# Context keys and values of a decoder layer: seven-product projections on two positions side by side, 512 columns each, and values turned by VectorE when they are loaded

## The chip, the cores and the metric

The kernel runs on one core of one Trainium2 chip. The metric is device time in microseconds (us) for one execution. The engines are named as in the profile: PE (TensorE, matrix products; PEld is its loading of the stationary operand), DVE (VectorE), ACT (ScalarE), POOL (GpSimd), SP (SyncE, which here issues most transfers). SBUF is the memory on the core, PSUM the memory that PE writes its sums to.

## What is computed

One decoder layer over 8 positions t of 512 rows each: self-attention across the positions, cross-attention to a context, and a small network, each followed by an addition and a layer norm. The change concerns the context's keys and values:

```python
x = layernorm(x + self_attention(x, ...))                    # 8 positions x 512 rows x 512
# cross-attention: ctx is 8 x 512 rows x 1024 features
src_trans = einsum('bsf,of->bso', ctx, W_src) + b_src        # W_src: 1024 x 1024
src_trans = src_trans * mask[:, :, None]
k, v = split(src_trans, 2, axis=2)                           # 8 heads of 64
q = (einsum('btf,of->bto', x, W_tgt) + b_tgt) * mask[:, :, None]
scores = where(mask == 0, -inf, einsum('bthd,bshd->bhts', q, k) / 8)
update = einsum('bhts,bshd->bthd', softmax(scores), v)
x = layernorm(x + einsum('btf,of->bto', concat(x, update), W_out) + b_out)
x = layernorm(x + network(x))                                # rounded to a small float format
```

All data that concern the change are 32-bit floats.

## The kernel before

**Two halves.** The first half (to line 617) does self-attention and the context's keys and values; the second half does cross-attention and the network. They meet in DRAM: normalized rows in `x1d`, keys in `kd`, values in `vd`, one tensor for each position.

**First half, main work.** A loop over j, four blocks of 128 rows; in each block all 8 positions t. PE projects keys, queries and values (`ps_k`, `ps_q`, `ps_v`, line 338) from `xt`, and a bias term `bd` (line 369). DVE forms the scores (lines 379 and 388, `pq` and `sc`) and the weighted values (lines 428 to 444, `pv` and `ao`). PE turns the result (`aot`, line 449) and applies the output projection (`po`, line 454). The input rows are loaded again into `r` (line 463, pool `rp`, 5 buffers), POOL adds a bias, DVE adds `po`, takes statistics and normalizes four positions at a time, and ACT's queue stores the rows to `x1d`.

**First half, context products.** For positions 0 to 6 the projection is done with seven block products in place of eight (lines 482 to 617). W_src's half for keys (part 0) or for values (part 1) is cut in 2 x 2 blocks, 256 outputs by 512 features. The context of one position, transposed (features on partitions), is cut in 2 x 2 blocks as well: `cl` and `ch`, the lower and the upper 512 features, by two halves of 256 rows. `halves` loads four blocks of W_src into one tile `w` and DVE forms three sums in it (`sums_of_a`, lines 136 to 139). `context_of` loads `cl` and `ch`, DVE forms the sums `tx` (`sums_of_b`, lines 142 to 145), and in part 0 the sums are stored to DRAM (`td`), so that part 1 loads them and doesn't form them again. In part 0 the stationary operand is a block of `w` and 256 columns of context move, giving keys transposed. In part 1 the stationary operand is a block of context and 256 columns of `w` move, giving values with rows on partitions. `product` (line 535) makes four matmuls over the four feature chunks. Three banks `py`, `pz`, `px` take the sums; ACT (`put`) writes a bank to the staging tile `st`, adding the bias or multiplying by the mask, and DVE (`add`) adds another bank to it (lines 587 and 589). The order of the seven products is A12, S1, A11, S2, S4, S3, A22. The staging tiles go to `kd` and `vd` from ACT's queue.

The scheduler mixes these products with the main work by its own estimates; on each engine the resulting order is fixed. Position 7 is projected plainly (`project_context`, eight groups of eight matmuls, lines 151 to 187), by a matrix `w_src` that is loaded at the start of the second half.

**Buffers that matter.** `big` holds one tile: `w` of part 0, then `w` of part 1, then `w_src`, then the network's `w1`. A tile can be loaded when the last reader of the one before it is done. `cxp` has 10 buffers of 2 KB a partition for `cl` and `ch`, 8 for each position; `tcp` has 5 of 3 KB for `tx`, 4 for each position. `kst` has 4 staging buffers, `ps_kv` three PSUM banks.

**Second half.** Here the order on PE, DVE, ACT and SP is written out by hand: `weave` sets steps of attention between dense products, and smaller works of DVE wait in the lists `urgent` and `side`, which `run` empties by a credit as PE's steps go by. A list `later` holds loads that go out a number of steps later. For each position t and each of four column chunks c (two heads), `scores` makes the scores (line 782), DVE and ACT form the softmax (lines 797 to 822), DVE turns 32x32 blocks into `pb` (line 834), sixteen transfers on SP's queue put these in place as `pT` (line 847), and `attend` multiplies by the values `v` (line 881). `load_v` fetches the values of one chunk with one transfer, two chunks ahead (`kvd` has 2 buffers). `queries`, `project_x1`, `project_u`, `hidden` and `finish` are the dense products.

Of the kernel before, what the change touches and what calls it, by code (L numbers as in the profile page):

```python
# [42 lines left out]
def decoder_layer(  # L43
# [145 lines left out]
    with ExitStack() as ph:  # L189
# [136 lines left out]
        rp = ph.enter_context(tc.tile_pool(name="rp", bufs=5))  # L326
        sm = ph.enter_context(tc.tile_pool(name="sma", bufs=2))
        cxp = ph.enter_context(tc.tile_pool(name="cxp", bufs=10))
        tcp = ph.enter_context(tc.tile_pool(name="tcp", bufs=5))
# [17 lines left out]
        for j in range(NJ):  # L347
# [134 lines left out]
        HF, W2 = FC // 2, S // 2  # L482
        td = [
            [dram.tile([P, 5, W2], F32, name=f"td{t}_{f}") for f in range(HF)]
            for t in range(T - 1)
# [13 lines left out]
        def context_of(t, part):  # L499
            lo, hi, tx = [], [], []  # L500
            for f in range(HF):
                a = cxp.tile([P, S], F32, tag="ct", name=f"cl{part}{t}_{f}")
                b = cxp.tile([P, S], F32, tag="ct", name=f"ch{part}{t}_{f}")
                x = tcp.tile([P, 3, W2], F32, tag="tx", name=f"tx{part}{t}_{f}")
                nc.sync.dma_start(b, ctxT[t, (HF + f) * P : (HF + f + 1) * P, :])
                if part == 0:
                    nc.sync.dma_start(a, ctxT[t, f * P : (f + 1) * P, :])
                    with tc.high_priority():
                        sums_of_b(
                            nc.vector,  # L510
                            *(u[:, h * W2 : (h + 1) * W2] for u in (a, b) for h in (0, 1)),
                            *(x[:, i] for i in range(3)),
                        )
                    nc.sync.dma_start(td[t][f][:, 0:2], a)
                    nc.sync.dma_start(td[t][f][:, 2:5], x)
                else:
                    nc.sync.dma_start(a, td[t][f][:, 0:2])
                    nc.sync.dma_start(x, td[t][f][:, 2:5])
                lo.append(a)
                hi.append(b)  # L520
                tx.append(x)
            return lo, hi, tx

        for part in range(2):
            w7 = halves(part)
            for t in range(T - 1):
                lo, hi, tx = context_of(t, part)
                first, second = slice(0, W2), slice(W2, S)
                b11, t3 = [u[:, first] for u in lo], [u[:, second] for u in lo]
                b21, b22 = [u[:, first] for u in hi], [u[:, second] for u in hi]  # L530
                t1, t2, t4 = ([u[:, i] for u in tx] for i in range(3))
                for i in range(2):
                    ps = slice(i * P, (i + 1) * P)

                    def product(bank, a, b, start):


                        for f in range(HF):
                            nc.tensor.matmul(  # L539
                                bank[:, first],  # L540
                                lhsT=w7[:, a, f, ps] if part == 0 else b[f][:, ps],
                                rhs=b[f] if part == 0 else w7[:, a, f, :],
# [5 lines left out]
                    def bank(name):  # L548
                        return ps_kv.tile(
                            [P, S], F32, tag="kv", name=f"{name}{part}{t}_{i}"  # L550
# [3 lines left out]
                    st = [  # L554
                        kst.tile([P, S], F32, tag="st", name=f"st{part}{t}_{i}_{k}")
                        for k in range(2)
                    ]
                    at = {}
                    for r in range(2):
                        for c in range(2):  # L560
                            k, q = (r, c) if part == 0 else (c, r)
                            at[r, c] = k, st[k][:, (first, second)[q]]

                    def put(r, c, src):


                        k, dst = at[r, c]
                        n = i + 2 * k
                        with tc.high_priority():
                            if part == 0:  # L570
                                nc.scalar.activation(
                                    dst, src[:, first], AF.Identity, bias=col(C_BK + n)
                                )
                            else:
                                nc.scalar.activation(
                                    dst,
                                    src[:, first],
                                    AF.Copy,
                                    scale=maskcol[:, t, n : n + 1],
                                )  # L580

                    def add(r, c, src):
                        k, dst = at[r, c]
                        n = i + 2 * k
                        with tc.high_priority():
                            if part == 0:
                                nc.vector.tensor_tensor(dst, src[:, first], dst, ALU.add)
                            else:
                                nc.vector.scalar_tensor_tensor(
                                    dst,  # L590
                                    src[:, first],
                                    maskcol[:, t, n : n + 1],
                                    dst,
                                    ALU.mult,
                                    ALU.add,
                                )
# [9 lines left out]
                    add(0, 0, x)  # L606
                    product(x, S2, t2, False)
                    put(0, 1, x)
                    product(z, S4, b22, False)
                    add(0, 1, z)  # L610
                    product(x, S3, t3, False)
                    add(1, 1, x)
                    product(x, A22, t4, False)
                    put(1, 0, x)
                    for k in range(2):
                        d = (kd, vd)[part][t]
# [683 lines left out]
```

## Time and profile before

| | |
|---|---|
| three runs, median (lowest to highest) | 2162.68 us (2159.54 to 2164.2) |
| the profiled execution, its own time | 2161.87 us |
| its span, first to last instruction | 2160.1 us |
| L539, context products | 1568 records, 366.6 us busy |
| L338, `ps_k`, `ps_q`, `ps_v` | 768 records, 342.3 us busy |
| L428, DVE, weighted values | x64, mean 2320 ns |
| L834, DVE, 32x32 turns | x256, mean 678 ns |
| L143, DVE, a sum of context, 256 columns | x28, mean 607 ns |
| mean granted PE clock | 0.989 |

The profile is of one execution. A stage is a stretch of the span in microseconds from its start. For each engine the busy time in a stage is given; PEclk is the clock granted to PE as a share of full speed; the DMA share is that of the core's 16 DMA engines. An f32 product stands as two records. The last `po` of the first half ends at 873.6 us, the last context product at 922.9, and the first query product of the second half starts at 922.7.

### The profile page before, as it was taken

What the parts mean: (1) busy time and instruction counts of PE and PEld (TensorE: products, weight loads), DVE (VectorE), ACT (ScalarE), POOL (GpSimd) and SP (SyncE); (2) the same over time, 40 slices, a digit from 0 to 9 for tenths busy, and PEclk for the clock granted to TensorE, in tenths of its full rate; (3) what the DMA queues carried; (4) which work ended last, traced back from release to release, by engine and by line L of the source; (5) the groups of instructions that cost most, each with busy time, mean ns of one, the idle gap of its engine ahead of it and who ended that gap; (6) DMA issues with size and microseconds to landing.
All of it is one profiled execution on the core that took longest, in us unless ns stands there. A gap on an engine that the chain in (4) does not pass through costs nothing.

```text
span 2160.1 us, 19078 instructions
## 1 busy us (share of the span) xinstructions
PE 2080.1 (96%) x6544; PEld 1040.1 (48%) x6544; DVE 1453.5 (67%) x2378; ACT 479.8 (22%) x1011; POOL 143.7 (7%) x124
## 2 busy tenths in 40 slices
PE   7999999999999999997899999999999999999998
PEld 5564665466446666742343444444443434343443
DVE  3799998999999989255663574754735638456232
ACT  2012111110211121122223233232232322323211
POOL 1000110011001101000000001000010000000000
PEclk9999999999999999998999999999999999999999
DMA  8130343044324224984495572744744628336200
GB/s 287 67 127 15 134 172 132 6 141 151 93 67 158 88 98 146 283 232 130 105 211 123 107 143 72 131 113 98 132 117 99 145 67 147 103 83 141 64 20 20
DMA packets 253297, 257.48 MB, mean 119 GB/s; under 512 B 141456, under 2 KB 161936, under 8 KB 253200
## 3 DMA queue, kind: packets, MB, share of 16 engines
q1 hardware_dynamic: 236976, 227.65, 41.7%
q10 hardware_dynamic: 16224, 28.61, 3.6%
q8 instruction: 52, 0.85, 0.2%
q14 instruction: 45, 0.37, 0.1%
HBM read 129.84 MB, written 59.24 MB: 88 GB/s over the span
## 4 chain that ended last, share of the span: by engine, by line
PE 75%; DVE 16%; DMA 5%; issue 1%; SPq 1%; ACT 1%; POOL 0%; ACTq 0%; DVEq 0%
PE h L970 21%; PE px L539 7%; PE pox L915 5%; PE av L881 5%; PE s L782 5%; PE pox L903 5%; PE psq L762 4%; PE o L987 4%; DVE pv L428 4%; PE pz L539 4%; PE ps_q L338 3%; PE po L454 2%; DVE pv L438 2%; DVE sc L388 2%; DVE pq L379 2%; PE py L539 2%
## 5 line engine op out<-in xcount | busy, mean ns | idle before, releaser
L970 PE MATMUL h<-x2T,w 128*128 128x512 f32 x1024 | 454.7, 599 | 4.5 <-DVE x2T L726 4.5
L970 PEld LDWEIGHTS h<-x2T,w 128*128 128x128 f32 x1024 | 192.2, 191 | 263.4 <-issue 253.9
L797 DVE CUSTOM_DVE_ANT_0 pe<-s,mb 128x512 f32<-128x512 f32 x256 | 162.0, 682 | 218.2 <-PE s L782 218.2
L807 ACT ACTIVATE pe<-pe,nmax 128x512 f32<-128x512 f32 x256 | 182.2, 712 | 217.6 <-DVE nmax L797 215.7
L834 DVE STREAM_TRANSPOSE pb<-pe 128x512 f32<-128x512 f32 x256 | 159.6, 678 | 0.0
L977 ACT ACTIVATE hq<-h,colv 128x512 fp8e4<-128x512 f32 x128 | 88.0, 687 | 302.4 <-PE h L970 302.4
L428 DVE TENSOR_TENSOR pv<-v,sc 128x2048 f32<-128x2048 f32 x64 | 148.5, 2320 | 2.0
L379 DVE TENSOR_TENSOR pq<-qw,k 128x2048 f32<-128x2048 f32 x64 | 146.6, 2291 | 1.1
L388 DVE TENSOR_REDUCE sc<-pq 128x64 f32<-128x2048 f32 x64 | 146.0, 2281 | 1.4
L782 PE MATMUL s<-kT,qTx 64*128 64x512 f32 x512 | 128.9, 620 | 4.3 <-DVE nmax L797 4.1
L881 PE MATMUL av<-pT,vx 128*64 128x512 f32 x512 | 119.2, 608 | 8.9 <-DMA pT<-pb 8.9
L762 PE MATMUL psq<-x1Ts,w_tgt 128*128 128x512 f32 x256 | 117.0, 610 | 5.8 <-DVE x1Ts L726 5.8
L822 DVE TENSOR_SCALAR pe<-pe,rden 128x512 f32<-128x512 f32 x256 | 116.9, 499 | 4.5
L454 PE MATMUL po<-w_o,aoT 128*128 128x512 f32 x256 | 117.4, 601 | 0.8 <-ACT aoT L451 0.8
L338 PE MATMUL ps_q<-w_in,xt 128*128 128x512 f32 x256 | 116.8, 594 | 0.0
L915 PE MATMUL pox<-w_xo,uT 128*128 128x512 f32 x256 | 115.2, 598 | 0.0
L903 PE MATMUL pox<-w_xo,x1Ts 128*128 128x512 f32 x256 | 114.4, 595 | 0.0
L987 PE MATMUL o<-w2q,hq 128*128 128x512 fp8e4 x512 | 114.1, 379 | 0.0
L338 PE MATMUL ps_k<-w_in,xt 128*128 128x512 f32 x256 | 113.9, 593 | 0.1
L338 PE MATMUL ps_v<-w_in,xt 128*128 128x512 f32 x256 | 111.6, 594 | 0.0
L922 DVE TENSOR_TENSOR x<-pox,x 128x512 f32<-128x512 f32 x32 | 22.1, 692 | 107.9 <-PE pox L915 60.2
L900 POOL TENSOR_TENSOR x<-x,bxo 128x512 f32<-128x512 f32 x32 | 39.9, 1279 | 817.7 <-DMA x<-x1d 318.6
(153 smaller groups left out, 2397.3 us busy)
## 6 DMA issues: line engine op xcount, KB each, us to landing
pT<-pb SPq DMA_DIRECT2D x512, 128.0 KB, 2.3
ch<-in_ctxT_dram SPq DMA_DIRECT2D x56, 256.0 KB, 3.4
td<-tx SPq DMA_DIRECT2D x28, 384.0 KB, 3.2
tx<-td SPq DMA_DIRECT2D x28, 384.0 KB, 5.0
r<-in_x_dram SPq DMA_DIRECT2D x32, 256.0 KB, 3.6
xt<-in_xT_dram SPq DMA_DIRECT2D x32, 256.0 KB, 2.7
x1d<-r ACTq DMA_DIRECT2D x32, 256.0 KB, 3.5
x1Ts<-x1d SPq DMA_DIRECT2D x32, 256.0 KB, 5.9
```

What stands on the lines that cost most here:

```text
L338: nc.tensor.matmul(ps, lhsT=xt[:, e, :], rhs=w_in[:, e, part * E : (part + 1) * E], start=(e == 0), stop=(e == EC - 1),)
L379: nc.vector.tensor_tensor(pr, qw[:, fs] .rearrange("p (h d) -> p h d", d=D1) .unsqueeze(2) .to_broadcast([P, HH, T, D1]), k_all[:, :, fs]. ...
L388: nc.vector.tensor_reduce(sc[:, t, g * HH * T : (g + 1) * HH * T], pr.rearrange("p h s d -> p (h s) d"), AX.X, ALU.add,)
L428: nc.vector.tensor_tensor(pr, v_all[:, :, fs].rearrange("p s (h d) -> p s h d", d=D1), sc[:, t, g * HH * T : (g + 1) * HH * T] .rearrange( ...
L539: nc.tensor.matmul(bank[:, first], lhsT=w7[:, a, f, ps] if part == 0 else b[f][:, ps], rhs=b[f] if part == 0 else w7[:, a, f, :], start=st ...
L762: nc.tensor.matmul(ps, lhsT=w_tgt[:, e, o * P : (o + 1) * P], rhs=x1T[t][:, e, :], start=(e == 0), stop=(e == EC - 1),)
L782: nc.tensor.matmul(ps[:, h, :], lhsT=qT[t][half[h], c, j * P : (j + 1) * P], rhs=kT[t, c][half[h], :], start=True, stop=True,)
L881: nc.tensor.matmul(av[half[h], :], lhsT=v[t, c][:, s, half[h]], rhs=pT[t, c][:, :, :, s, h].rearrange("p g i q -> p (g i) q"), start=(s == 0),
L903: nc.tensor.matmul(po, lhsT=x1T[t][:, e, j * P : (j + 1) * P], rhs=w_xo[:, e, :], start=(e == 0), stop=False,)
L915: nc.tensor.matmul(po, lhsT=uT[t][:, e, j * P : (j + 1) * P], rhs=w_xo[:, EC + e, :], start=False, stop=(e == EC - 1),)
L970: nc.tensor.matmul(ps, lhsT=w1[0][:, e, n * P : (n + 1) * P], rhs=x2T[t][:, e, :], start=(e == 0), stop=(e == EC - 1),)
L987: nc.tensor.matmul(po, lhsT=hq[t][:, c, j * P : (j + 1) * P], rhs=w2q[:, c, :], start=(c == 0), stop=(c == HC - 1),)
```

## The change

- Positions 0 to 5 are taken in three pairs. The 2 x 2 blocks of context are now the lower and upper features by the two positions of a pair, so every product moves 512 columns. There are 336 of them, where there were 784 with 256 columns.
- In part 1, too, the stationary operand is a block of `w`. Values therefore come out transposed, like the keys, with features on partitions and rows as columns, and are stored so. When a bank is written to `st`, its 32-column blocks are reordered.
- Every result block has a staging tile of its own (four for each step, from the same four buffers) and is stored when it is complete.
- The mask and the turning of the values move to the second half: `load_v` fetches a raw chunk in four transfers, `turn_v` has DVE turn 32x32 blocks and POOL multiply by the mask. The work is put in the list `side`, one chunk ahead.
- Position 6 is projected plainly like position 7, at the end of the first half, by `w_src`, whose load moves there from the second half.
- `cxp` has 8 buffers of twice the size and `tcp` 4 of twice the size, one pair's worth each; `rp` has 4.

```diff
-        rp = ph.enter_context(tc.tile_pool(name="rp", bufs=5))
+        rp = ph.enter_context(tc.tile_pool(name="rp", bufs=4))
...
-        cxp = ph.enter_context(tc.tile_pool(name="cxp", bufs=10))
-        tcp = ph.enter_context(tc.tile_pool(name="tcp", bufs=5))
+        cxp = ph.enter_context(tc.tile_pool(name="cxp", bufs=8))
+        tcp = ph.enter_context(tc.tile_pool(name="tcp", bufs=4))
...
-        def context_of(t, part):
+        def context_of(m, part):
...
-                a = cxp.tile([P, S], F32, tag="ct", name=f"cl{part}{t}_{f}")
-                b = cxp.tile([P, S], F32, tag="ct", name=f"ch{part}{t}_{f}")
-                x = tcp.tile([P, 3, W2], F32, tag="tx", name=f"tx{part}{t}_{f}")
-                nc.sync.dma_start(b, ctxT[t, (HF + f) * P : (HF + f + 1) * P, :])
+                a = cxp.tile([P, 2, S], F32, tag="ct", name=f"cl{part}{m}_{f}")
+                b = cxp.tile([P, 2, S], F32, tag="ct", name=f"ch{part}{m}_{f}")
+                x = tcp.tile([P, 3, S], F32, tag="tx", name=f"tx{part}{m}_{f}")
...
+                nc.sync.dma_start(b, two(HF + f))
...
-            for t in range(T - 1):
-                lo, hi, tx = context_of(t, part)
-                first, second = slice(0, W2), slice(W2, S)
-                b11, t3 = [u[:, first] for u in lo], [u[:, second] for u in lo]
-                b21, b22 = [u[:, first] for u in hi], [u[:, second] for u in hi]
+            for m in range(PAIRS):
+                lo, hi, tx = context_of(m, part)
+                b11, t3 = [u[:, 0] for u in lo], [u[:, 1] for u in lo]
+                b21, b22 = [u[:, 0] for u in hi], [u[:, 1] for u in hi]
...
-                                bank[:, first],
-                                lhsT=w7[:, a, f, ps] if part == 0 else b[f][:, ps],
-                                rhs=b[f] if part == 0 else w7[:, a, f, :],
+                                bank,
+                                lhsT=w7[:, a, f, i * P : (i + 1) * P],
+                                rhs=b[f],
...
+                            else:
+                                nc.scalar.copy(order(st[r, c], "g s e"), order(src, "s g e"))
...
+                            nc.vector.tensor_tensor(dst, order(src, "s g e"), dst, ALU.add)
...
+        w_src = big.tile([P, FC, 2 * E], F32, tag="big", name="w_src")
+        for h in range(2):
+            es = slice(h * E, (h + 1) * E)
+            nc.sync.dma_start(w_src[:, :, es], chunked(w_srcT)[:, :, es])
+        t = T - 2
+        ct6 = []
+        for i in range(FC // 2):
+            ct6.append(cxp.tile([P, 2, S], F32, tag="ct", name=f"ct6{i}"))
+            nc.sync.dma_start(ct6[i], chunked(ctxT[t])[:, 2 * i : 2 * i + 2, :])
+        for piece in project_context(
+            t, w_src, lambda f: ct6[f // 2][:, f % 2, :], ps_kv, "kv", kst, "st"
+        ):
+            piece()
...
+        def load_v(p):
+            t, c = p // EC, p % EC
...
+            raw[p] = kvd.tile([P, 4, P], F32, tag="raw", bufs=1, name=f"raw{p}")
+            for g in range(4):
+                nc.sync.dma_start(
+                    raw[p][32 * g : 32 * g + 32],
+                    vd[t][:, c, g * P : (g + 1) * P].rearrange("(b r) q -> r b q", r=32),
+                )
+
+        def turn_v(p):
...
             v[t, c] = kvd.tile([P, ST, P], F32, tag="v", name=f"vx{t}_{c}")
-            nc.sync.dma_start(v[t, c], vd[t][:, :, c * P : (c + 1) * P])
+            nc.vector.transpose(
+                v[t, c].rearrange("p s (b e) -> p b s e", e=32),
+                raw[p].rearrange("p b (s e) -> p b s e", e=32),
+            )
+            nc.gpsimd.tensor_tensor(
+                v[t, c],
+                v[t, c],
+                maskcol[:, t, :].unsqueeze(2).to_broadcast([P, ST, P]),
+                ALU.mult,
+            )
+            if p + 1 < (T - 2) * EC:
+                later.append([2, lambda: load_v(p + 1)])
+
+        def turn_v_soon(p):
+            if p < (T - 2) * EC:
+                side.append((("v", p), 0.7, lambda: turn_v(p)))
...
             settle((t * EC + c) * 2 + 1)
+            settle(("v", t * EC + c))
...
             p = t * EC + c + 2
-            if p < T * EC:
-                later.append([2, lambda: load_v(p // EC, p % EC)])
+            if p >= (T - 2) * EC:
+                later.append([2, lambda: load_v(p)])
+            turn_v_soon(p - 1)
...
-                    w_src = big.tile([P, FC, 2 * E], F32, tag="big", name="w_src")
-                    for h in range(2):
-                        es = slice(h * E, (h + 1) * E)
-                        nc.sync.dma_start(w_src[:, :, es], chunked(w_srcT)[:, :, es])
```

## The prediction

> **What bounds the kernel now.** I read the page's engine totals first, then the busy times cut into stages, then the projection's own instructions in the same stages, then the timeline where the first half hands over to the second, and last the waits there.
>
> ```profile
> PE 2080.1 (96%) x6544; PEld 1040.1 (48%) x6544; DVE 1453.5 (67%) x2378; ACT 479.8 (22%) x1011; POOL 143.7 (7%) x124
> ```
>
> TensorE (PE) is busy 96% of the span. But the stages differ (columns: us, busy us of each engine, clock, DMA share, GB/s):
>
> ```profile
> core 0: us, PE busy (x) PEld busy (x) DVE busy (x) ACT busy (x) POOL busy (x), PEclk, DMA share, GB/s
> 235.00:347.00 112.00, 104.01 (x426) 78.03 (x424) 108.69 (x127) 12.81 (x27) 14.92 (x11) 0.97 0.46 165
> 449.00:547.00 98.00, 92.49 (x366) 65.92 (x365) 92.69 (x100) 10.39 (x22) 9.95 (x8) 0.97 0.44 155
> 764.00:875.00 111.00, 106.32 (x428) 75.45 (x427) 99.23 (x115) 19.31 (x36) 7.89 (x7) 1.00 0.45 148
> 875.00:923.00 48.00, 45.83 (x200) 37.83 (x199) 10.02 (x22) 6.92 (x16) 5.57 (x4) 0.96 0.88 258
> ...
> 1100.00:1200.00 100.00, 100.00 (x274) 40.49 (x274) 49.84 (x122) 31.22 (x68) 8.38 (x6) 1.00 0.66 161
> ```
>
> In the first half VectorE (DVE) and PE are almost equally full; from 875 to 923 PE alone works, on context products left over; from 1100 PE has no idle time and DVE is half idle. The context products (L539) in those first-half stages together, and the timeline of the handover:
>
> ```profile
> sum 886.00, PE 366.59 PEld 296.00; mean PE 40.73 PEld 32.89
> ```
> ```profile
> 905.45 1.89 PE L539 MATMUL pz<-w,ch 128*128 128x256 f32 x8
> 907.18 1.89 PE L539 MATMUL px<-w,cl 128*128 128x256 f32 x8
> ...
> 922.73 13.90 PE L762 MATMUL psq<-x1Ts,w_tgt 128*128 128x512 f32 x32
> ...
> 939.92 3.70 PE L160 MATMUL psk<-ct7a,w_src 128*128 128x512 f32 x8 [1.37 <-DMA ct7a<-in_ctxT_dram]
> ```
>
> Each f32 product is two records. Eight records of 256 columns go from 905.45 to 907.18: 1.73 us, 0.216 each, so 0.432 us a product. The 32 records of 512 columns take 13.90 us with the tail of the last (about 0.15), 0.43 each, 0.86 us a product. Width buys nothing: two narrow products cost 0.864.
>
> **The change part by part.**
>
> *Products.* Before: 7 positions x 2 parts x 2 x 7 x 4 = 784 narrow products, 784 x 0.432 = 338.7 us. After: 3 pairs x 2 x 2 x 7 x 4 = 336 wide ones, 289.0 us, and position 6 plain, 8 x 8 = 64 wide, 55.0 us. Sum 344.0: PE gets 5.3 us more work, since position 6 loses its saving of an eighth.
>
> *Where they stand.* In the changed program's order on PE the paired products, counted up to the last value projection of each of the four position blocks, then to the last output projection (po_7), then after it, are 30, 75, 78, 67, 82 and 4; before they are 88, 168, 134, 130, 162 and 102. Up to po_7 that is 332 x 0.86 = 285.5 against 682 x 0.432 = 294.6: 9.1 us less. After po_7: 4 wide and then all 64 of position 6, against 102 narrow.
>
> *The tail.* Before, from po_7's end (873.6) to the first query product (922.7) is 49.1 us: 102 x 0.432 = 44.1 and short waits. After: 4 x 0.86 = 3.4, then a wait, then 55.0. The wait is new: w_src takes the room of the seven sums (pool big holds one tile), so its load starts when the last paired product ends, and the plain products need its first half at once. Before, that load lay under 16 query products and 2 of scores. On SP's queue, in order, stand ahead of it ct6 (2.10 MB), w_tgt (1.05) and w_xo (2.10); ct6 waits for tiles that the third product from the end (S3) frees, 9.0 us before that end (2 x 0.86 of S3, one transposition pair 0.41, po_7 3.44, last product 3.44). With the half of w_src (2.10) that is 7.34 MB. How fast:
>
> ```profile
> w_src<-in_w_srcT_dram SPq DMA_DIRECT2D x2, 2048.0 KB, 11.3
> ```
> ```profile
> DMA to landing us min/median/max: 8.8/11.3/13.8
> ```
>
> (the median of w_src's two loads, issued at 922.9, and the spread of the two). At 345 GB/s, what the stretch from 923 to 940 moved, 7.34 MB take 21.3 us; at the 258 of 875 to 923, 28.5. Less 9.0, that is 12 to 20 us of wait; below, w_src alone is 8.8; above, stores of about 2 MB (x1d, vd) that run then add 8: 28. I take 17, nearer the upper rate since little else reads then. After such a stop the clock is down: the stretch 960 to 980, with 6.68 us idle, shows 0.96 and 1000 to 1020 shows 0.90, together 2.8 us of clock; I take 2 (0 to 3). Tail: 3.4 + 17 + 2 + 55.0 = 77.4 against 49.1, +28 (bounds +18 to +40).
>
> *Buffers.* cxp goes from 10 tiles of 2 KB for 8 a position to 8 of 4 KB for 8 a pair, tcp from 5 to 4: nothing of the next pair is loaded while this one is used. Second part: a pair is 7.34 MB (hi 2.10, lo 2.10, sums 3.15), 28 us at 258 GB/s; hi and lo come free by S3, the sums only with the last product. From S3 to the pair's first product with sums PE has S3, the last product, the next first one (3.4 each) and one or two projections of the main stage (3.4 each): 14 to 17 us, so 5 to 7 us of wait at a switch after the first arrivals. Four such switches, 24 us, take the place of 12 smaller ones, and PE's idle ahead of L539 groups now sums to 23 (of that, 22.1 us of waits in both PE queues are on ch loads). Net +3, bounds -15 and +26. rp from 5 to 4 delays the r load of t = 4 behind a store (3.5 us) and a load (3.6); 9.6 us of DVE products (2 x 4.77) cover it. The first loads are 0.5 MB bigger ahead of xt, 2 us.
>
> The Trainium skill, "Trainium Kernel Development and Optimization", Best Practices, asks for double buffers so that transfers overlap with compute. By that rule the four switches would each show their first 4.2 MB, 16 us at the 258 GB/s above, less one product: some 50 us in place of my 24, and the sum would be 26 higher. The trace's waits at today's switches are far under a whole transfer, so I go by them.
>
> *DVE in the first half.* Sums: 112 narrow instructions (L142 to L145), 15.5 + 15.8 + 10.7 + 10.3 = 52.3 us, become 48 of 512 columns; L997's 692 ns gives 33, twice the narrow means 48. Adds: 84 (L587, L589), 37.6 us, become 36 x 0.685 (L470) = 24.7. Saving 17 to 32, take 25. PE waits on DVE ahead of aot for 12.7 us in all; I let 3 of it go. ScalarE's 112 copies of 0.475 become 48 of about 0.6: 53 to 29 us, on an engine at 22%, nothing.
>
> *Second half.* 24 times: four SP issues for raw where one was (0.6 us each, 1.8 more; they stand behind 16 pT issues that take 10 of about 39 us a unit, and kT waits behind them, needed a unit later), one VectorE transposition (L834, 0.678: 16.3 us; twice that if the pattern costs), one GpSimd multiplication by the mask (1.28 at L900 to 1.69 at L464: 31 to 40). A load for p+1 goes out a unit before its turn, a turn a unit before its use; DVE has 50 of 100 us free, PE 0. Cost 0. Without that cover it is 24 x (0.68 + 1.69) = 57.
>
> The Trainium skill, "SBUF — State Buffer", Who interferes with whom, says that a DVE instruction with two SBUF inputs and a GpSimd one that reads SBUF lock each other out. By it the 24 multiplications could hold DVE up for 31 to 40 us more; the sum stays the same as long as DVE's free half covers it, and no row here has such a multiplication beside a full DVE in the second half.
>
> *Handover.* The second half's start now suffers from full queues:
>
> ```profile
> 961.52 17.06 SPq L847 DMA_DIRECT2D pT<-pb  x16
> ...
> 1028.22 10.05 SPq L847 DMA_DIRECT2D pT<-pb  x16
> ```
>
> The first 16 pT issues took 7 us longer than later ones, and PE waited 6.68 for them at 980.7. With w_src and the x1T loads done under 55 us of products, I take 5 back (bounds -12, and +6 if the first turns and multiplications stand in that chain).
>
> *Sum* on the profiled execution's 2161.9 (span 2160.1): -9.1 +2 +3 -3 +28 -5 = +16: 2178. The median of the runs is 0.8 higher: **2179**.
>
> **Rivals.** *DVE is the real bound of the first half* (108.69 of 112). Then its 25 us come off, not the 7 of PE's side: 2162.7 - 25 + 28 - 5 = 2161, and with the tail's wait at 12 and the handover at -10, 2151; 2156 in the middle: faster. For it: DVE's fill. Against: in 235 to 347 PE's 104 leaves it 8 us, not 25, and the stages where DVE alone leads (138 to 235) hold 3.7 us of context products. It decides if PE's waits for aot and the sums vanish. 13%. *Starved switches*: each shows a whole first reload of 4.2 MB, 26 us over mine, and the tail's wait is at 27, +10: 2215, slower. For it: no spare tile. Against: today's short waits. 17%. *The wait for w_src is hidden or replaced*: the loads ahead of it finish early and the wait is 5: 2167. Against: it cannot start before the last product. 8%. *The turns show*: PE waits for v at half the units, 12 x 2.4 = 29: 2208. Against: a unit of lead. 5%. The forecast itself, 2165 to 2198, has 57%.
>
> A measurement of this kernel tells about 0.2% (4.3 us) from no change. Faster by more: most of the first rival and a little of the third, 12%. Within: 8%. Slower: 80%. The range that holds 8 of 10: 2157 to 2208; the forecast's own is 2165 to 2198.
>
> **What would show it.** L544 records at 0.43 apart; a gap of 12 to 20 us ahead of the first psk, ended by w_src or ct6, and 55 us of plain products before the first query; po_7's end near 866; waits of 5 to 7 us at four switches; PE still at 100 of 100 in the second half with L783 at about 0.68 us. It is wrong if po_7 ends before 850 (DVE was the bound) or after 890 (starved), or if PE idles in the second half ahead of av.

## The result and the profile after

| | before | after |
|---|---|---|
| median of 20 runs each | 2160.43 us | 2168.04 us |
| lowest to highest | 2156.24 to 2164.71 | 2164.43 to 2170.5 |
| span of the profiled execution | 2160.1 us | 2166.1 us |

The ratio is 1.0033, with a 95% interval of 1.0026 to 1.004: the change makes the kernel slower by 7.6 us. The forecast was slower by 16, at 2179 in a range of 2157 to 2208. The side was right and the time lies in the range, but the loss is less than half of what was forecast, and the terms of the sum show larger errors than their total.

The engine totals of the changed kernel:

```profile
PE 2079.9 (96%) x5776; PEld 892.7 (41%) x5776; DVE 1439.7 (66%) x2290; ACT 464.7 (21%) x955; POOL 167.5 (8%) x148
```

PE does the same work in fewer, wider records. Where the time lies is read in three stretches, cut at the end of the last output projection of the first half (po_7) and at the first query product. First the context products up to po_7, by the four position blocks and the last rest; columns are start and end, length, PE busy and weight loads of those products alone, clock, DMA share, GB/s. The changed kernel (L544):

```profile
0.00:154.30 154.30, 27.48 (x60) 11.25 (x60) 1.00 0.46 161
154.30:348.10 193.80, 67.27 (x150) 27.62 (x150) 1.00 0.31 109
348.10:554.60 206.50, 73.54 (x156) 29.85 (x156) 0.98 0.35 124
554.60:745.10 190.50, 61.69 (x135) 25.75 (x136) 0.99 0.22 76
745.10:852.80 107.70, 74.54 (x165) 29.55 (x165) 1.00 0.41 142
sum 852.80, PE 304.51 PEld 124.03; mean PE 60.90 PEld 24.81
```

The same view of the kernel before (L539), its sum only:

```profile
sum 873.80, PE 319.67 PEld 257.72; mean PE 63.93 PEld 51.54
```

po_7 ends at 852.8 in place of 873.7: 20.9 us earlier, where 7 were forecast. The records are 0.43 us apart, as expected. Then the tail, in the timeline of PE:

```profile
849.12 3.70 PE L454 MATMUL po<-w_o,aoT 128*128 128x512 f32 x8
852.66 3.60 PE L544 MATMUL px<-tx,w 128*128 128x512 f32 x8
869.47 29.76 PE L160 MATMUL psk<-ct,w_src 128*128 128x512 f32 x64 [13.22 <-DMA w_src<-in_w_srcT_dram]
899.07 27.63 PE L174 MATMUL psv<-w_src,ct 128*128 128x512 f32 x64
926.54 5.74 PE L809 MATMUL psq<-x1Ts,w_tgt 128*128 128x512 f32 x13
```

Four products, a wait of 13.22 us for w_src, 57 us of position 6, and the first query product at 926.5: 73.7 us after po_7, where the kernel before had 49.0. The loss of 24.7 answers the forecast of 28. The load that PE waits for, with the median and the spread of the time from issue to landing of its two halves:

```profile
w_src<-in_w_srcT_dram SPq DMA_DIRECT2D x2, 2048.0 KB, 15.0
```
```profile
DMA to landing us min/median/max: 12.5/15.0/17.5
```

Last, the second half, from the first query product to the end: 1239.6 us, against 1237.4 before. The forecast was 5 us less. SP's queue around its start, and a stretch later on in which PE had no idle time before (columns as in the stages of the prediction):

```profile
902.34 14.08 SPq L772 DMA_DIRECT2D raw<-vd  x4
...
931.86 8.57 SPq L731 DMA_DIRECT2D x1Ts<-x1d  x4
...
954.69 7.16 SPq L772 DMA_DIRECT2D raw<-vd  x4
964.62 16.00 SPq L894 DMA_DIRECT2D pT<-pb  x16
```
```profile
1104.00:1204.00 100.00, 96.61 (x259) 38.71 (x258) 49.21 (x119) 30.61 (x68) 8.06 (x7) 0.98 0.76 166
```

The first pT issues got only 1 us shorter (16.00 against 17.06), and PE now stops in 1104 to 1204. Three of its stops, with what ended them:

```profile
982.48 5.51 PE L929 MATMUL av<-pT,vx 128*64 128x512 f32 x16 [6.12 <-DMA pT<-pb]
...
1111.83 7.13 PE L809 MATMUL psq<-x1Ts,w_tgt 128*128 128x512 f32 x16 [1.39 <-DVE x1Ts L737]
...
1145.99 5.35 PE L929 MATMUL av<-pT,vx 128*64 128x512 f32 x16 [2.00 <-DMA raw<-vd]
```

The last, a stop ahead of av that the raw values end, is one that the prediction had named as a sign of being wrong.

| term | forecast, us | measured, us |
|---|---|---|
| paired products up to po_7, by their number | -9.1 | -9.1 (332 x 0.86 against 682 x 0.432) |
| first loads, switches, VectorE: +2 +3 -3 | +2 | -11.8 |
| tail, po_7 to the first query product | +28 | +24.7 |
| second half | -5 | +2.2 |
| sum on the spans | +16 | +6.0 |

So two questions are open: why the first half gained 14 us more than forecast, and why the second half did not gain. The experiments were each timed beside the kernel before on the same chip; ratios are to it. Places within a trace are those of one execution: in the eight traces whose first half is the changed kernel's up to its last loads, po_7 ends anywhere from 850.6 to 856.6, so a difference of a few us in po_7 says little by itself.

### The profile page after: what moved, and what is told of

Read it like the earlier page. It is cut to its first block, busy times and chain, and to the rows that moved or that the text cites. A ratio compares the mean times of both kernels' runs of the same rounds, so it can differ in the third digit from the quotient of the medians.

```text
span 2166.1 us, 17275 instructions
## 1 busy us (share of the span) xinstructions
PE 2079.9 (96%) x5776; PEld 892.7 (41%) x5776; DVE 1439.7 (66%) x2290; ACT 464.7 (21%) x955; POOL 167.5 (8%) x148
## 4 chain that ended last, share of the span: by engine, by line
PE 67%; DVE 24%; DMA 5%; issue 2%; ACT 1%; POOL 0%; SPq 0%; ACTq 0%; DVEq 0%; POOLq 0%
PE h L1018 21%; PE s L829 5%; PE psq L809 5%; PE pox L963 5%; PE pox L951 5%; PE av L929 5%; DVE pq L379 5%; DVE sc L388 5%; PE o L1035 4%; PE px L544 4%; DVE pv L428 3%; PE psk L160 3%; PE psv L174 2%; DVE pv L438 2%; PE pz L544 2%
## 5 line engine op out<-in xcount | busy, mean ns | idle before, releaser
L544 PE MATMUL px<-tx,w 128*128 128x512 f32 x192 | 92.1, 604 | 4.2 <-DVE st L586 4.2
```

Of the source, the lines that this page charges most:

```text
L544: nc.tensor.matmul(bank, lhsT=w7[:, a, f, i * P : (i + 1) * P], rhs=b[f], start=start and f == 0, stop=f == HF - 1, skip_group_check=not s ...
```

## The experiments

### Four on the first half and the tail

*Position 6 first* (six_first):

```diff
+w_src = big.tile(...)          # and ct6, project_context(6, ...)
 for part in range(2):
     w7 = halves(part)
...
-w_src = big.tile(...)          # and ct6, project_context(6, ...)
...
 if t == 0:
+    w_src = big.tile([P, FC, 2 * E], F32, tag="big", name="w_src7")
+    for h in range(2):
+        es = slice(h * E, (h + 1) * E)
+        nc.sync.dma_start(w_src[:, :, es], chunked(w_srcT)[:, :, es])
```

> The changed kernel with position 6 projected first instead of last: w_src whole at the start, then the three pairs, and w_src loaded a second time under the first queries, as the kernel before loads it. Theory (the tail's wait is a pure loss of order: 13.2 us in which PE waits for w_src, and 2 of clock): after po_7 stand 72 wide products, 72 x 0.86 = 61.9 us, with no wait in front, against 73.7 in the changed kernel; before po_7 stand 4 products fewer, 3.4 us. 2168.0 - 13.2 - 2 = 2153, between 2150 and 2157, faster than both kernels. Rival (the wait moves): the load of the seven sums' sources must then wait for position 6's last product, PE finds no context products in the second block, which lengthens by 10 us or more, and the total is 2162 to 2168.

2170.7 us, ratio 1.0043 (1.003 to 1.0055): the theory fell. The wait for w_src did go, and the tail took 67.8 us in place of 73.7. But the loss came back at two places. Before po_7 there are 8 wide products fewer (324 against 332, 6.9 us), and yet po_7 ends at 852.7, as in the changed kernel. Two stops stand there that the changed kernel does not have: 3.27 us ahead of the first `ps_k`, behind larger first loads, and 4.69 at 284.8, where the list of waits names w, the sources of the seven sums; after both the clock is lower (0.95 in 30 to 100 us, 0.97 in 100 to 348, where it was 1.00). That is the rival's wait, though smaller than its 10 us. And the second load of w_src stood among the loads in front of the pT transfers:

```profile
852.70:920.50 67.80, 63.84 (x145) 26.42 (x144) 11.49 (x20) 5.57 (x10) 3.64 (x3) 1.00 0.68 213
920.50:987.50 67.00, 55.25 (x137) 22.50 (x136) 31.87 (x77) 15.74 (x36) 4.56 (x3) 0.94 0.74 211
```

In the second row, from the first query product to the first av, PE is busy for 55 of 67 us; in the changed kernel this stretch is 55.9 us long. The kernel before loads w_src there too and has 58.0, so w_src alone does not make the 67: four context products that came behind the first query product (3.4 us) and the raw loads stand there as well, and the shares are not told apart. Position 6 last keeps w_src out of this place; what that is worth by itself is not shown.

*w_src in eight pieces* (pieces):

```diff
-for h in range(2):
-    es = slice(h * E, (h + 1) * E)
+for h in range(8):
+    es = slice(h * P, (h + 1) * P)
     nc.sync.dma_start(w_src[:, :, es], chunked(w_srcT)[:, :, es])
```

> The changed kernel with w_src loaded in eight pieces of 128 columns (0.5 MB each) where it has two of 512. Theory: the first plain product needs the first piece alone; w_src's second half lands 5.0 us after its first, so 2.1 MB pass in 5 us and the first piece lands 3.75 us before the half did: wait 13.2 - 3.75 = 9.5 us, total 2164 (2163 to 2166). Each further piece has 6.9 us of products ahead of it and needs 1.25. Rival: what the wait pays is the 5.2 MB queued ahead of w_src and the latency, or pieces with rows of 512 bytes move slower: the wait stays at 12 or grows, total 2167 to 2173.

2165.21 us, ratio 1.002 (1.0012 to 1.0029), as the theory had it. The wait in the timeline is 10.11 us, 3.1 less.

*The old kernel with the new buffer counts* (old_cut_buffers), the change's first four numbers alone:

```diff
-rp = ... bufs=5    cxp = ... bufs=10    tcp = ... bufs=5
+rp = ... bufs=4    cxp = ... bufs=8     tcp = ... bufs=4
```

> The kernel before with the change's buffer counts alone (cxp 8 for 10, tcp 4 for 5, rp 4 for 5): nothing of the next position is loaded while this one is used. By the prediction's step (a switch without spare tiles waits 5 to 7 us for a pair of 7.34 MB, so some 3 us for a position of 3.67 MB) the 12 switches cost 36 us, less what they cost now: 2175 to 2195. Rival, formed from the result (main-stage products fill the switches, the spare tiles were worth almost nothing): 2158 to 2165.

2180.07 us, ratio 1.0086 (1.0071 to 1.01). By the total the prediction's step looks right, but the place shows it wrong. Up to po_7 there are 664 narrow products in place of 682 (7.8 us), and po_7 ends at 867.6, 6.1 earlier: without spare tiles the first half is 1.7 us longer, over 11 switches, which is less than po_7 varies from trace to trace. The rest comes after po_7, where PE has no other work to go to:

```profile
867.60:935.80 68.20, 57.17 (x234) 44.07 (x233) 11.77 (x24) 7.89 (x17) 3.64 (x3) 0.95 0.76 236
```

116 narrow products, 50.1 us by their number, took 68.2; before, 102 took 49.0. That is 13 us more than the 14 additional products explain. The start of the second half, behind the same late loads, lost another 8. The Trainium skill, "Trainium Kernel Development and Optimization", Best Practices, asks for double buffers so that transfers overlap with compute; here this agrees where the context products stand alone (13 us) and not where the main stage covers them (1.7 us, within the spread).

*VectorE's work split* (dve_split):

```diff
-eng.tensor_tensor(t1, b12, b11, ALU.subtract)          # four sums, 512 columns
+for h in (slice(0, S // 2), slice(S // 2, S)): ...     # the same four, 256 columns
...
-nc.vector.tensor_tensor(dst, order(src, "s g e"), dst, ALU.add)
+for q in (0, 1): nc.vector.tensor_tensor(d, u, d, ALU.add)     # each half
```

> The changed kernel with each sum over the context (L142 to L145) and each addition (L586) done in two VectorE instructions of 256 columns, as wide as they were before: 48 more at 0.467 us for 34.2 us of sums and 36 more at 0.448 for 24.6 of additions, 18 us of VectorE work more, no more data. By the prediction (12.7 us of PE waits for aot, of which 3 in 25 follow VectorE's load): +2, 2168 to 2172. Rival (VectorE sets the length of the first half, so what po_7 came too early, 14 us, is VectorE's relief): +12 to +18, 2180 to 2186, with po_7's end at 865 or later.

2168.52 us, ratio 1.0036 (1.0022 to 1.0049), the changed kernel's time. The groups of VectorE's instructions show 67.8 us for sums and additions against 58.8, so 9 us came back, not 18, out of the 31 that the change had taken off (89.9 in the kernel before). po_7 ended 1.2 us earlier, not 9 later, and the total did not move. So VectorE's relief is not where the 14 us come from, as far as these 9 of 31 us tell.

### Width, switches and the values' way

*Narrow products in the changed kernel* (narrow_products):

```diff
-nc.tensor.matmul(bank, lhsT=w7[...], rhs=b[f], ...)
+for q in range(2):
+    h = slice(q * S // 2, (q + 1) * S // 2)
+    nc.tensor.matmul(bank[:, h], lhsT=w7[...], rhs=b[f][:, h], ...)
```

> The changed kernel with each paired product of 512 columns issued as two of 256, as narrow as they were before: 672 products in place of 336, every load, sum, addition and buffer as in the changed kernel. By the prediction's rule (width buys nothing: 2 x 0.432 against 0.86) 336 x 0.004 = 1.3 us more: 2167 to 2171. Rival (width is what brought po_7 14 us earlier than forecast: the narrow records pay 0.104 us after every stop of PE and half the clock longer, and each wait on a load comes twice as often): 2176 to 2184.

2167.58 us, ratio 1.0028 (1.0016 to 1.004): the prediction's rule holds, width buys nothing. po_7 ends at 844.4, with 645 narrow products ahead of it where the changed kernel's 332 wide ones are worth 664: 19 fewer, 8.2 us, and the difference to 852.8 is 8.4.

*Twice the switches* (switch_double):

```diff
-for m in range(PAIRS):
-    lo, hi, tx = context_of(m, part)
-    ...
-    for i in range(2):
+for i in range(2):
+    for m in range(PAIRS):
+        lo, hi, tx = context_of(m, part, i)
```

> The changed kernel with the loop over the two column blocks outside the loop over the pairs: each part goes through the three pairs twice, so there are 12 switches of the context's tiles where there were 6, with the same 336 wide products, buffers and sums; the second pass of the first part reloads the sums as the second part does (7.34 MB a pair, 44 MB more in all). Theory (a switch costs, beside what the main stage covers: in the changed kernel 16 us of PE's idle ahead of context products before po_7 and 9 us of clock, nearly all at its 5 switches, in the kernel before 21 and 15 at its 11 or 12, so 3 to 5 us each; pairing gained by halving their number): po_7's end 15 to 25 us later, and the total 2182 to 2196. Rival (switches are covered, and what pairing gained lies in the chains of products and their evictions): 2166 to 2172.

2172.82 us, ratio 1.0063 (1.005 to 1.0075). The stretch from 30 us to po_7, of the kernel before, the changed one and this one (columns: PE, weight loads, DVE, ACT, POOL):

```profile
30.00:873.80 843.80, 808.03 (x2780) 492.18 (x2780) 776.06 (x769) 115.48 (x211) 73.98 (x64) 0.99 0.33 112
```
```profile
30.00:852.80 822.80, 792.99 (x2080) 356.96 (x2080) 752.70 (x668) 100.92 (x161) 73.22 (x64) 0.99 0.32 111
```
```profile
30.00:857.50 827.50, 790.77 (x2072) 357.35 (x2072) 750.52 (x667) 100.49 (x161) 72.77 (x64) 0.99 0.46 161
```

With 328 products ahead of po_7 in place of 332 (3.4 us), po_7 comes 4.7 us later: 8.1 us for six switches more, 1.35 each, with all the additional loading in it (161 GB/s against 111). Measured against the whole spread of po_7 in the changed kernel, it is 4.3 to 10.3 us, 0.7 to 1.7 a switch. The size lies below the theory, which had 15 to 25; the total is just above the rival's range. Among the waits ahead of L544 that name a cause, the loads now lead (us of idle time of both PE queues, number of stops):

```profile
  DMA tx<-td: 17.7, 16
  DMA w<-in_w_srcT_dram: 10.0, 2
  DMA ch<-in_ctxT_dram: 8.6, 6
```

In the changed kernel the waits on loads there are 9.3 us on tx<-td, in 6 stops, 3.1 on w, in one, and none on ch; in the kernel before ch alone has 20.8, in 12.

*No turns* (no_turns), *no mask* (no_mask) and *turns aside* (turns_aside):

```diff
 def load_v(p):
-    if t >= T - 2:
+    if True:                       # no_turns, turns_aside: v in one load
...
-nc.gpsimd.tensor_tensor(v[t, c], v[t, c], maskcol[...], ALU.mult)     # no_mask: out
...
-side.append((("v", p), 0.7, lambda: turn_v(p)))
+side.append((("v", p), 0.7, lambda: turn_aside(p)))   # turns_aside: into a tile of its own
...
-    if p < (T - 2) * EC:
+    if False:                      # no_turns: no turn and no mask
...
+load_v(1)                          # no_turns, turns_aside: a second chunk ahead
...
-settle(("v", t * EC + c))          # no_turns, turns_aside: av does not wait for a turn
```

> The changed kernel whose second half loads the values of positions 0 to 5 in one piece, with neither the turn on VectorE nor the multiplication by the mask on GpSimd, so that these positions attend to values that are not turned back; two value tiles are loaded ahead, as in the kernel before. By the prediction (turns cost 0 in the second half, the first ones up to 6 at its start): 2164 to 2169, and the stretch from the first query product to the end within 3 us of 1239.6. Rival (the turns are why the handover's 5 us did not come): 2157 to 2162, with the first av 5 us or more earlier.

2157.99 us, ratio 0.999 (0.998 to 1.0): the rival held. The values' new way costs 10 us, where the prediction put 0.

> The changed kernel without the multiplication of positions 0 to 5's turned values by the mask on GpSimd; the raw loads and VectorE's turns stay. Theory (the loads in front of pT cost the start of the second half, not the engines): 2166 to 2169. Rival (GpSimd's 24 multiplications of 1.040 us, between the turn and av, or their port, cost the 10 us that went without turns): 2158 to 2163.

2168.96 us, ratio 1.0042 (1.0029 to 1.0056): the multiplication of 1.040 us on GpSimd costs nothing.

> The run without turns (values of positions 0 to 5 in one load, attended to unturned), with the 24 VectorE turns and the 24 GpSimd multiplications put back at their old places, but into a tile that nobody reads: av waits for neither. Theory (the loads in four pieces, not the engines, cost the 10 us): 2157 to 2160, like the run without turns. Rival (the turn on VectorE, ahead of the exponentials of the next scores, costs it): 2164 to 2169, like the changed kernel.

2157.4 us, ratio 0.9986 (0.9977 to 0.9995). With all 24 turns and multiplications running, the time is that of the run without them. What costs is the way of loading, then (four pieces, one chunk ahead in place of two), or that av waits for the turn. Where, is seen from the first query product to the eighth av, the changed kernel first, then turns_aside:

```profile
926.50:1215.20 288.70, 267.53 (x705) 105.59 (x703) 161.78 (x384) 78.60 (x180) 25.32 (x20) 0.96 0.61 139
```
```profile
927.80:1204.30 276.50, 263.67 (x705) 104.63 (x703) 161.70 (x384) 78.60 (x180) 28.81 (x22) 0.98 0.60 145
```

The same 705 records take 12.2 us less, 3.9 of it in the length of the records and the rest in stops; after the eighth av the difference stays (950.9 us to the end against 952.0). So the cost lies in the first two positions' work. From there on a unit takes 35.4 us in both.

### Versions that try to mend it

*w_tgt and w_xo late* (pieces_late), on top of the eight pieces:

```diff
-nc.sync.dma_start(w_tgt, chunked(w_tgtT))     # ahead of w_src on SP
-nc.sync.dma_start(w_xo, chunked(w_xoT))
...
 load_x1T(0)
+nc.sync.dma_start(w_tgt, chunked(w_tgtT))
+nc.sync.dma_start(w_xo, chunked(w_xoT))
```

> The run with w_src in eight pieces, and w_tgt and w_xo (3.15 MB) loaded behind w_src and x1T in place of ahead of them. Theory (w_src's wait is the queue ahead of it: w_xo, issued at 846.5, lands 15.5 us later, at 862, when w_src has been issued for 5 us): the first piece lands 5 us earlier, wait 9.5 - 5 = 4.5, total 2160 (2157 to 2162), level with the kernel before. Rival (the wait is latency, or w_tgt now is late for the first query product): 2164 to 2170.

2158.12 us, ratio 0.9988 (0.9978 to 0.9999). The wait falls to 5.21 us:

```profile
859.21 30.57 PE L160 MATMUL psk<-ct,w_src 128*128 128x512 f32 x64 [5.21 <-DMA w_src<-in_w_srcT_dram]
```

So most of the 13.22 us was the 3.15 MB queued in front of w_src and the size of its first half.

*The second values earlier* (raw_early) and *x1T later* (x1t_late), both on top of that:

```diff
 load_v(0)
+load_v(1)                                    # raw_early: into a tile of the pool sp
...
-load_x1T(1)                                  # x1t_late: behind the first pT
-load_x1(0)
+dense.insert(6, of(0.0, load_x1T, 1)[0])
+dense.insert(7, of(0.0, load_x1, 0)[0])
```

> The run with w_src in pieces and w_tgt and w_xo late, and the values of the second pair of heads of position 0 loaded before the first query product, into a tile of the pool of exponentials, in place of ahead of the first 16 pT issues; all later turns stay as they are. Theory (without turns the first 16 pT issues took 11.8 us in place of 16.0, and the first av came 4.8 us earlier: the four raw loads stand ahead of pT in a queue that is already full): the first av 3 to 5 us earlier, total 2153 to 2155, faster than every version so far. Rival (the turn on VectorE or the mask on GpSimd holds the start up): 2157 to 2160.

2158.12 us, ratio 0.9992 (0.9982 to 1.0001): nothing gained. pT's first issues still took 16.15 us (from 960.89), with no raw load left between them and x1T's loads (from 928.42). So the raw loads ahead of pT are not what makes its first issues long, nor is it the place of the second chunk.

> The run with w_src in pieces and w_tgt and w_xo late, and position 1's x1T (four loads in rows of 128 bytes, 8.6 to 13.8 us to issue) and position 0's x1 loaded behind the first 16 pT issues in place of ahead of them. Theory (what makes the first pT issues take 16 us in place of 10 is the x1T load in the queue ahead): pT issued in 10 to 12 us, the first av 4 to 6 us earlier, total 2152 to 2155. Rival (x1T now is late for the first queries of position 1, or queues ahead of the second pT): 2157 to 2163.

2159.49 us, ratio 0.9993 (0.9981 to 1.0005): nothing gained, but the mechanism shows. The first pT issues went out fast, with four raw loads just ahead of them that took 1.88 us, and the second ones, now behind x1T, were slow; PE stopped for 0.99 us at the first av and 9.91 at the second, where pieces_late has 6.55 at the first.

```profile
958.65 10.69 SPq L892 DMA_DIRECT2D pT<-pb  x16
...
974.54 10.96 SPq L729 DMA_DIRECT2D x1Ts<-x1d  x4
...
987.71 15.94 SPq L892 DMA_DIRECT2D pT<-pb  x16
```

*Values stored ready for one load* (raw_plain), on top of pieces_late:

```diff
+vt = [dram.tile([EC, 4, 32, 4, P], F32, name=f"vt{t}") for t in range(T - 2)]
...
-nc.scalar.dma_start(vd[2 * m + c][:, i + 2 * r, :], st[r, c])      # part 1
+for b in range(4):
+    nc.scalar.dma_start(vt[2 * m + c][i + 2 * r][:, :, b, :].rearrange("g r q -> r g q"),
+        st[r, c][32 * b : 32 * b + 32].rearrange("r (g q) -> r g q", g=4))
...
-for g in range(4):
-    nc.sync.dma_start(raw[p][32 * g : 32 * g + 32], vd[t][:, c, g * P : (g + 1) * P]...)
+nc.sync.dma_start(raw[p], vt[t][c].rearrange("g r b q -> (g r) b q"))
```

> The run with w_src in pieces and w_tgt and w_xo late, and the transposed values stored so that the load ahead of a turn is one issue of 128 rows of 2 KB in place of four issues of 512-byte pieces; a store in the second part becomes four (72 more issues on ScalarE's queue in the first half). Turns and masks stay. Theory (the form of the raw loads costs the start of the second half its 10 us): the stretch from the first query product to the end falls from 1239.2 to about 1230, total 2148 to 2152, the fastest version. Rival (any load at that place costs it, because it waits for room that position 6's products hold, and the loads in one piece only came through in another order): 1236 to 1240, total 2156 to 2161. The first half as in that run, unless the stores in four pieces hold the context's evictions up: then po_7's end is later than 855.

2151.23 us, ratio 0.9964 (0.995 to 0.9978): the theory held, and this version is faster than both kernels. Its SP queue at the same place, the first av, and the stretch to the eighth av:

```profile
903.97 0.42 SPq L776 DMA_DIRECT2D raw<-vt  x1
...
919.51 8.25 SPq L736 DMA_DIRECT2D x1Ts<-x1d  x4
...
949.02 0.50 SPq L776 DMA_DIRECT2D raw<-vt  x1
959.00 11.31 SPq L895 DMA_DIRECT2D pT<-pb  x16
```
```profile
972.16 3.65 PE L930 MATMUL av<-pT,vx 128*64 128x512 f32 x16 [1.43 <-DMA pT<-pb]
```
```profile
920.90:1197.50 276.60, 263.68 (x705) 104.63 (x703) 161.73 (x384) 78.60 (x180) 26.81 (x21) 0.98 0.56 138
```

The turns and masks are all there, and av waits for them, yet the stretch is as short as without them; from the first query product to the end it is 1228.6 us. The four issues in front of the first query product, 14.08 us in the changed kernel, have become one of 0.42; the next four, 7.16 us in front of pT, one of 0.50.

The time of these issues is not itself what PE loses. In turns_aside two loads at the first place took 19.83 us, and its second half is one of the short ones; and pT's first issue comes 38.1 us after the first query product both in the changed kernel and in raw_plain. What goes with the loss is the place of the loads of x1T, position 1's rows (x1Ts in the profile). Eight traces, the changed kernel's among them, have the values in four pieces and these loads ahead of pT (six_first, with w_src among them, is left out). Their second halves take 1238.3 to 1239.6 us, and in all of them x1T's loads start 5.0 to 5.6 us after the first query product (931.86 against 926.54). no_turns, turns_aside and raw_plain have 1228.3 to 1228.6, and there they start 1.4 to 2.6 us before it (919.51 against 920.91). The first pT issues then take 11.2 to 11.8 us in place of 16.0 to 16.2. That fewer issues of values let x1T's loads out earlier is the likely way; no run moves x1T's loads forward alone, so it is not shown. The stores in four pieces did not hold the first half up: po_7 ends at 854.6.

## Why the prediction was right in sign and wrong in size

*The first half: the step that failed.* "5 to 7 us of wait at a switch after the first arrivals. Four such switches, 24 us, take the place of 12 smaller ones", net +3. It priced a switch by the bytes to be reloaded less the one or two projections nearest to it. (Its own figures, 24 less the 23 of today, make +1, not +3.) The runs put a switch of a pair at 1.35 us (8.1 for six more; 0.7 to 1.7 by the spread of po_7), and the spare tiles that were taken away at 1.7 us for the whole first half, no more than the spread. The likely reason is that the scheduler puts main-stage work into a switch as long as there is any: where none was left, in old_cut_buffers behind po_7, missing spare tiles cost 13 us. So fewer switches are a gain, not a loss: from 12 to 5 ahead of po_7, 7 x 1.35 = 9.5 us of the 11.8 that "first loads, switches, VectorE" came to, 5 to 12 with the spread. This is an estimate, since the 1.35 was measured on the changed kernel's switches, and those of the kernel before are half as large. Why the first half gained all of its 11.8 us stays open to that extent. PE's idle fell by 6.0 us (843.80 - 808.03 against 822.80 - 792.99). Its busy time fell by 15.0, 9.1 by the number of products; the remaining 5.9 is in the length of the records, slower ones after stops among them, which the prediction had not counted at all. VectorE's share, 3 us, is too small for dve_split to show, and the rule on width was right (narrow_products).

*The tail* was right as a mechanism, and its sizes lay within their bounds: wait 13.2 for 17 in bounds of 12 to 20, clock 2.1 for 2 (psk's 64 records took 29.76 us, psv's 27.63), the whole 24.7 for 28. Pieces and pieces_late show the queue ahead of w_src as the cause that the step named.

*The second half: two errors in one term.* "Cost 0" for the turns held for the engines (turns_aside, no_mask) and for the steady state. It failed for the loads at the start: the step counted 1.8 us of issues on SP behind pT, by the pace of later issues, and not the queue in front of the first pT, with x1T's loads in it. The four-piece loads cost 1239.6 - 1228.6 = 11 us there. Up to the eighth av the changed kernel loses 12.1 us against raw_plain: 4.7 in the stop at the first av (6.12 against 1.43), 3.4 in the two stops at 1111.83 and 1145.99, which raw_plain does not have, and 3.9 in the length of the records. "Take 5 back" for the handover was right in direction and too small: with the values in one load (turns_aside, raw_plain) the second half is 1237.4 - 1228.6 = 8.8 us shorter than before. The sum of both is the +2.2. The step that failed for the handover is "the x1T loads done under 55 us of products": position 1's went out from 931.86, 5.3 us after the first query product, and stood ahead of pT again. The bound of +6 held by luck: it named turns and multiplications in that chain, which turns_aside and no_mask clear.

*The total.* It lies only some 10 us from the forecast because errors of -14, -3 and +7 us partly cancel; that is luck, and the range, 51 us wide, would have held each of them alone.

*The rivals.* VectorE as the real bound fell in dve_split, though po_7 at 852.8 came close to the 850 that was named for it; an early po_7 spoke for fewer switches as well, which no rival held. Starved switches fell: 1.35 us each. The wait for w_src was hidden in no run: it was shortened, or in six_first it moved. The turns that show came true in one sign, PE's stop ahead of av at 1145.99, but not by the turns and not at half the units: 11 us in place of 29, by the loads, at the start only.

## What to carry to other kernels

Price a buffer switch by what other work stands ready for the engine there, not by the bytes: without spare tiles the old kernel lost 1.7 us, no more than one trace differs from the next, over 11 switches beside a main stage and 13 where nothing stood beside them. Where two phases meet, the order and the form of loads on one queue decide: there four small issues in place of one cost 11 us, and from the eighth av on the same issues cost nothing. Before a place within one trace is explained, see how far it moves in traces of the same code. Check each term against its own stretch of the trace, since errors of -14, -3 and +7 us here added up to a total that looked nearly right.

## What the hardware showed

Issue time on SP depends on what stands ahead: four raw loads of 64 KB took 14.08 and 7.16 us at the start of the second half and about 1.9 later, sixteen pT issues 16.0 when they began 33 us after x1T's loads did, 11.2 to 11.8 when 39 to 41 us after, and 10.0 in steady state. The Trainium skill, "DMA: Bandwidth & Descriptors", Rules for kernel authors, advises to coalesce many small transfers into a large one; raw_plain agrees, at a ratio of 0.9964 where pieces_late has 0.9988, though the row size and the number of issues changed together there and were not tried apart.

What the records lost after a stop of PE (granted clock 0.91 from 852.8 to 926.5) did not follow the stop's length: psk's 64 records took 29.76 us after 13.22 us of idle, 29.88 after 10.11 and 30.57 after 5.21, against 27.63 for the same number of psv records.
